# The way back from tokens to channels: 32x32 block transposes on VectorE in place of TensorE transposes, with x1 kept in another order of pixels

## The chip, the cores and the metric

The kernel runs on one core of a Trainium2 chip. The metric is the device time of one execution in microseconds (us). Before the change three runs took 6061.84, 6062.12 and 6064.63 us, median 6062.12. Five engines work side by side, each through a queue of its own in order: TensorE (PE in the profile; its weight loads are listed apart as PEld), VectorE (DVE), ScalarE (ACT), GpSimd (POOL) and SyncE (SP), which here issues the transfers. Semaphores tie them together: an instruction at the head of a queue that waits holds up everything behind it on its engine.

## The reference

The input is x, 32 images of 128 channels and 64x64 pixels, fp32. What is computed, cut to what matters:

```python
# layer 0: group norm, then a convolution by learned butterfly transforms
xc = complex(group_norm(x))
x_f = butterfly_along_h(butterfly_along_w(xc))      # 64-point transforms
prod = einsum('bihw,oihw->bohw', x_f, w_f)          # channels mixed at each frequency
x1 = x + real(inverse_butterflies(prod))

# layer 1: every pixel is a token of 128 channels
t = x1.reshape(B, C, H*W).transpose(0, 2, 1)
k, v = ln(t) @ Wk.T + bk, ln(t) @ Wv.T + bv          # ln: layer norm over channels
probs = softmax(einsum('sbe,sbf->sef', k, v) / sqrt(seq_len), axis=-1)
t = t + einsum('sef,sbf->sbe', probs, ln(t))         # one 128x128 matrix per image
p = softmax(ln(t) @ router_w + router_b)             # 8 experts, the best 2 are kept
t = t + sum(gate_of_the_two * (ln(t) @ expert_w[e] + expert_b[e]))
out = t.transpose(0, 2, 1).reshape(B, C, H, W)
```

The last line is the way back to channels.

## The kernel before

The kernel has three parts. Part one normalizes and transforms each image along w and h and writes the frequencies to DRAM (`xf`). Part two mixes channels, one column of frequencies after another, and writes `pf` to DRAM. Part three (lines 763 to 1390, from about 2600 us to the end) does all the rest, image by image, and the change lies there. 4096 pixels of an image make 32 tiles of 128 tokens, taken four at a time as groups g = 0 to 7.

For each image b, part three does the following. The names are those of the code and the profile.

- *Loads*, on SP's queue: eight tiles `r` of 256 KB from `pf` (line 856) and the image x itself, 2 MB (line 850, `y` in the profile).
- *Inverse transform.* Eight times PE makes `pu` in PSUM (line 877) and four ACT copies bring it into `u` (line 887); then PE makes `py` in four parts (line 899). `pu` and `py` share one PSUM buffer (room "cv"). For images 0 and 1 the same is done in smaller pieces in other buffers. For each `py`, `h_out` on DVE (line 907) adds PSUM to x in place. This makes x1, channels by pixels.
- *Front.* PE turns x1 into tokens, four 128x128 transposes per group into `pt` (line 1021); ACT copies `pt` into `tk[b % 2]` (line 1026), tokens by channels; DVE takes `bn_stats` (line 993) and combines them (moments, lines 1003 to 1008); POOL raises the variance to the power -1/2 (line 1013); a Gram matrix `pg` over all tokens (line 1072) and a softmax give the matrix of the attention; PE multiplies x1 by it (`pp`, line 1145), ACT scales, DVE adds to `tk` (line 1173).
- *Gate chain*, on DVE: router logits, the two largest, their weights (`logits1`, then `nmr2`, `logits2`, `first_max` twice, `second`, `between`, `gates`; lines 1204 to 1248, the last row is line 1248). It waits for a second power on POOL and has one exponential on ACT.
- *Experts*, for each group: ACT normalizes (`xn`, line 1273), PE turns (`px`, line 1283), ACT copies (`xT`, line 1289). For each of the 32 tiles two matmuls `pe` of 128x512 (line 1296; three PSUM buffers; the profile has two records for each) give eight experts' outputs; DVE multiplies each by the gates (`gated`, line 1307, here called m0_0, m0_1, ... by tile and half) into `tm` (two buffers, each a pair of tiles); POOL sums the experts and adds them to `tk` (lines 1332, 1333, 1335). In the last image five pairs are added by DVE directly (line 1319).
- *Way back*, for each group: `back(g)` is four PE transposes of `tk` into `po` (line 1342), `store(g)` is one ACT copy into `so` (line 1348) and one transfer of 256 KB to the output (line 1349).

`tk` has two buffers, so that the front of image b and the experts of image b - 1 or b - 2 run at the same time.

What sets the order is the class `Plan` (lines 25 to 87). Every step is handed to it with an engine, a supposed cost in us, a due time, the steps that must come before, and rooms that it takes and frees (the counts of buffers). The due time is 114 us times a position in the image's schedule, with a shift by the kind of step from the table `SHIFT` (line 826). Plan simulates the engines as list schedulers: a free engine takes the ready step with the earliest due time for which there is room. The instructions are then issued in exactly this order. A change of a cost, an engine, a room or a dependence can so change the order of any other step.

The steps that the prediction names are: `h`/`ho` (py and h_out), `pt`/`to`/`sa` (turn, copy, statistics), `va`, `pwa`, `na` (moments, power, and what follows it), `vb`, `pwb`, `lg`, `nb`, `l2`, `f1` to `f5`, `gt` (second norm and gate chain), `pe`/`m`/`s` (expert, gated, summed), `st`/`so` (way back).

Of the kernel before, what the change touches and what calls it, by code (L numbers as in the profile page):

```python
# [10 lines left out]
F32 = mybir.dt.float32  # L11
AF = mybir.ActivationFunctionType
ALU = mybir.AluOpType
# [3 lines left out]
P = 128  # L17
# [73 lines left out]
def kernel(  # L91
# [15 lines left out]
    nc = tc.nc  # L107
# [5 lines left out]
    n = HW  # L113
# [649 lines left out]
    eps = ctx.enter_context(tc.tile_pool(name="eps", bufs=3, space=PSUM))  # L763
    cps = ctx.enter_context(tc.tile_pool(name="cps", bufs=1, space=PSUM))
    tps = ctx.enter_context(tc.tile_pool(name="tps", bufs=3, space=PSUM))
    rp = ctx.enter_context(tc.tile_pool(name="rp", bufs=10))
    xp = ctx.enter_context(tc.tile_pool(name="xp", bufs=2))
    st = ctx.enter_context(tc.tile_pool(name="st", bufs=1))
    up = ctx.enter_context(tc.tile_pool(name="up", bufs=1))
    wp = ctx.enter_context(tc.tile_pool(name="wp", bufs=2))  # L770
# [13 lines left out]
    NG = 4  # L784
# [14 lines left out]
    def prepare():  # L799
# [20 lines left out]
        nc.tensor.matmul(pe[:, 0:NE], om, prx[0][:, P + NE : QX], start=True, stop=True)  # L820
        nc.vector.tensor_scalar_mul(rws, pe[:, 0:NE], float(P))

    plan = Plan({"cv": 1, "pe": 3, "tl": 3, "r": 10, "x": 2, "xg": NG, "xn": 2, "xT": 2, "tm": 2, "so": 2, "gate": 2})
    SLOT = 114.0

    SHIFT = {
        "ad": -0.15, "at": -0.25, "f": 0.71, "gs": -1.97, "gt": 0.71, "h": -0.24, "ho": -3.5, "kvp": 3.43,
        "kvq": -0.45, "l": 0.71, "lg": 3.61, "m": -0.32, "na": -1.87, "nb": -0.81, "pb": -1.97, "pc": -1.97,
        "pe": 0.16, "pg": -0.08, "pp": 0.19, "pr": -1.97, "prx": -1.97, "pt": -0.23, "pwa": -1.87, "pwb": 3.61,
        "px": 0.15, "r": -0.04, "s": 0.08, "sa": 1.29, "sm": -1.97, "sn": -1.97, "so": 2.13, "sr": -1.97,  # L830
        "st": 1.1, "t": -1.97, "to": 0.06, "va": -1.87, "vb": 3.61, "w": 0.28, "x": -0.68, "xT": -0.68,
        "xg": 0.21, "xn": 2.42,
    }
    made = {}
# [7 lines left out]
            engine, us, SLOT * at, run, [made[k] for k in names if k[0] >= 0], take, free, late  # L842
        )

    xs, rs, tile_of, first = {}, {}, {}, [prepare]

    def transfers(b):
        def load_x():
# [22 lines left out]
    def conv(b):  # L871
# [21 lines left out]
        def h_inverse(g):  # L893
# [7 lines left out]
                        )  # L901
            return run

        def h_out(g):
            def run():
                acc = xs[b][:, :, 16 * g : 16 * g + 16]
                nc.vector.tensor_tensor(
                    acc, tile_of.pop(("cy", b, g)).rearrange("o (w h) -> o h w", h=n), acc, ALU.add
                )
            return run  # L910


# [30 lines left out]

        def h_out_piece(q):
            def run():
                acc = xs[b][:, :, 8 * q : 8 * q + 8]
                nc.vector.tensor_tensor(
                    acc, tile_of.pop(("cz", b, q)).rearrange("o (w h) -> o h w", h=n), acc, ALU.add
                )
            return run  # L950

        if b < 2:
            for e in range(8):
                at = b + 0.08 * e
                for oh in range(2):
                    add(
                        b, f"w{e}_{oh}", "PE", 0.95, at + 0.04 * oh, w_inverse_piece(e, oh),
                        [f"r{e}"] + [(b - 1, f"h{k}") for k in range(4)], ("pe",), ("r",) if oh else (),
                    )
                    add(  # L960
                        b, f"wo{e}_{oh}", "ACT", 0.65, at + 0.04 * oh, w_out_piece(e, oh), [f"w{e}_{oh}"], (), ("pe",),
                    )
            for g in range(4):
                for k in range(2):
                    at = b + 0.68 + 0.07 * g + 0.035 * k
                    h, ho = (f"h{g}", f"ho{g}") if k else (f"h{g}_0", f"ho{g}_0")
                    add(
                        b, h, "PE", 1.05, at, h_inverse_piece(2 * g + k),
                        [f"wo{e}_{oh}" for e in range(8) for oh in range(2)] + ([f"h{g}_0"] if k else []), ("pe",),
                    )  # L970
                    add(b, ho, "DVE", 0.7, at, h_out_piece(2 * g + k), [h, "x"] + ([f"ho{g}_0"] if k else []), (), ("pe",))
            return
        for e in range(8):
            at = b + 0.08 * e
# [6 lines left out]
        for g in range(4):  # L981
            at = b + 0.68 + 0.07 * g
            add(b, f"h{g}", "PE", 2.05, at, h_inverse(g), [f"wo{e}_{oh}" for e in range(8) for oh in range(2)], ("cv",))
            add(b, f"ho{g}", "DVE", 1.2, at, h_out(g), [f"h{g}", "x"], (), ("cv",))

    def front(b):

# [27 lines left out]
        def turn(g):  # L1015
            def run():
                ps = tile_of["pt", b, g] = tps.tile([P, 512], F32, tag="tl", name=f"pt{b}_{g}")
                x1 = xs[b].rearrange("c h w -> c (h w)")
                for k in range(4):
                    i = 4 * g + k  # L1020
                    nc.tensor.transpose(ps[:, k * P : (k + 1) * P], x1[:, i * P : (i + 1) * P], ident)  # L1021
            return run
# [16 lines left out]
        s1 = b + 1  # L1039
        for g in range(8):  # L1040
            at = s1 + 0.016 * g
            add(b, f"pt{g}", "PE", 0.48, at, turn(g), [(b - 2, f"st{g}")] + [f"ho{k}" for k in range(4)], ("tl",))
            add(b, f"to{g}", "ACT", 0.55, at, turned(g), [f"pt{g}"], (), ("tl",))
            add(b, f"sa{g}", "DVE", 0.85, at, stats1(g), [f"to{g}"] + (["sa0"] if g else []))
        add(b, "va", "DVE", 1.7, s1 + 0.14, lambda: moments(1), [f"sa{g}" for g in range(8)])
# [92 lines left out]

        def product(lo, m):
            def run():  # L1140
                x1 = xs[b].rearrange("c h w -> c (h w)")
                ps = tile_of["pp", b, lo] = tps.tile([P, 512], F32, tag="tl", name=f"pp{b}_{lo}")
                for k in range(m):
                    i = lo + k
                    nc.tensor.matmul(  # L1145
                        ps[:, k * QX : (k + 1) * QX], x1[:, i * P : (i + 1) * P], prx[b % 2], start=True, stop=True
                    )
            return run
# [28 lines left out]
        for j, lo in enumerate(range(0, NT, 3)):  # L1177
            m = min(3, NT - lo)
            at = s1 + 0.45 + 0.016 * j
            add(b, f"pp{lo}", "PE", 0.26 * m, at, product(lo, m), ["prx", (b - 1, "lg")], ("tl",), ("x",) if lo == 30 else ())  # L1180
            add(
                b, f"at{lo}", "ACT", 0.4 * m + 0.2, at, scaled(lo, m),
                [f"pp{lo}"] + (["at0"] if lo else []),
            )
            add(
                b, f"ad{lo}", "DVE", 0.54 * m, at, added(lo, m),
                [f"at{lo}"] + (["ad0"] if lo else [f"pg{g}" for g in range(8)]), (), ("tl",),
            )
# [75 lines left out]
    def experts(b):  # L1264
# [70 lines left out]
                    nc.gpsimd.tensor_tensor(t[:, lo : lo + 2, :], t[:, lo : lo + 2, :], tm[:, :, m, :], ALU.add)  # L1335
            return run

        def back(g):
            def run():
                ps = tile_of["po", b, g] = tps.tile([P, 512], F32, tag="tl", name=f"po{b}_{g}")  # L1340
                for k in range(4):
                    nc.tensor.transpose(ps[:, k * P : (k + 1) * P], t[:, 4 * g + k, :], ident)
            return run

        def store(g):
            def run():
                so = wp.tile([P, 512], F32, tag="so", name=f"so{b}_{g}")
                nc.scalar.copy(so, tile_of.pop(("po", b, g)))
                nc.sync.dma_start(ov[b][:, g * 512 : (g + 1) * 512], so)
            return run  # L1350

        s2 = b + 2
        for g in range(8):
            at = s2 + 0.125 * g
            add(b, f"xn{g}", "ACT", 1.65, at - 0.1, normal(g), ["nb"], ("xn",))
            add(b, f"px{g}", "PE", 0.48, at - 0.05, turn(g), [f"xn{g}"], ("tl", "xT"), ("xn",))
            add(b, f"xT{g}", "ACT", 0.55, at - 0.05, turned(g), [f"px{g}"], (), ("tl",))
            for k in range(4):
                i = 4 * g + k
                for half in range(2):  # L1360
                    add(
                        b, f"pe{i}_{half}", "PE", 0.86, at + 0.125 * (2 * k + half) / 8, expert(i, half), [f"xT{g}"],
                        ("pe",), ("xT",) if k == 3 and half else (),
                    )
                    add(
                        b, f"m{i}_{half}", "DVE", 1.45 if i // 2 in direct else 0.64, at + 0.125 * (2 * k + half) / 8,
                        weighed(i, half) if i // 2 in direct else gated(i, half),
                        [f"pe{i}_{half}", "gt"] + ([f"m{i - k % 2}_0"] if k % 2 or half else []),
                        ("tm",) if k % 2 == 0 and half == 0 and i // 2 not in direct else (),
                        ("pe",) + (("gate",) if i == NT - 1 and half else ()),  # L1370
                    )
                if k % 2 and i // 2 in direct:
                    made[b, f"s{i // 2}"] = made[b, f"m{i}_1"]
                elif k % 2:
                    add(
                        b, f"s{i // 2}", "POOL", 5.5, at + 0.125 * (2 * k + 2) / 8, summed(i // 2),
                        [f"m{i - 1 + a}_{h}" for a in range(2) for h in range(2)], (), ("tm",),
                    )
            add(b, f"st{g}", "PE", 0.48, at + 0.25, back(g), [f"s{2 * g}", f"s{2 * g + 1}"], ("tl",))
            add(b, f"so{g}", "ACT", 0.55, at + 0.25, store(g), [f"st{g}"], (), ("tl",))  # L1380

    for b in range(B):
        transfers(b)
# [60 lines left out]
```

## Time and profile before

| | |
|---|---|
| profiled execution, span | 6062.4 us |
| median of three runs | 6062.12 us |
| PE busy | 5891.6 us, 97% |
| DVE, ACT, POOL busy | 4221.2, 3756.5, 4191.0 us |
| `po` transposes on PE (line 1342) | 155.0 us, 1024 records |
| `so` copies on ACT (line 1348) | 144.4 us, 256 |
| stores `out_dram<-so` | 256 of 256 KB, 2.2 us from issue to landing |
| loads `l<-xf` (part two, pieces of 512 B) | 1012 of 128 KB, 3.2 us |
| loads `r<-pf` | 504 of 256 KB, 4.7 us |
| load of x, `y<-in_x_dram` | 32 of 2 MB, 9.3 us |

The profile gives one span for the profiled execution, 6062.4 us, and no other time for it; it stands 0.3 us above the median of the runs. A row of a group reads: line, engine, operation, output<-input, size, count, then busy time in us and mean ns of one, then the idle time of the engine just ahead of these instructions and what ended most of it. In a time line the first number is the start in us and the second the duration; a bracket holds the idle time before it and its releaser. Matmuls are pipelined, so their durations overlap, and the time that one costs PE is better read from start to start.

### The profile page before, as it was taken

What the parts mean: (1) busy time and instruction counts of PE and PEld (TensorE: products, weight loads), DVE (VectorE), ACT (ScalarE), POOL (GpSimd) and SP (SyncE); (2) the same over time, 40 slices, a digit from 0 to 9 for tenths busy, and PEclk for the clock granted to TensorE, in tenths of its full rate; (3) what the DMA queues carried; (4) which work ended last, traced back from release to release, by engine and by line L of the source; (5) the groups of instructions that cost most, each with busy time, mean ns of one, the idle gap of its engine ahead of it and who ended that gap; (6) DMA issues with size and microseconds to landing.
All of it is one profiled execution on the core that took longest, in us unless ns stands there. A gap on an engine that the chain in (4) does not pass through costs nothing.

```text
span 6062.4 us, 219265 instructions
## 1 busy us (share of the span) xinstructions
PE 5891.6 (97%) x95372; PEld 4677.6 (77%) x95372; DVE 4221.2 (70%) x7696; ACT 3756.5 (62%) x7057; POOL 4191.0 (69%) x3765
## 2 busy tenths in 40 slices
PE   7999999999999999889999999999999999999998
PEld 7999999999999999776666666666666666666654
DVE  5565545555555555448878787787878878787878
ACT  7666664555555555366667667666766766676663
POOL 2110006666666666428898898989989898998988
PEclk9999999999999999999999999999999999999999
DMA  6767666666666666632313222231322223132100
GB/s 200 238 224 237 234 214 193 172 173 172 172 174 171 171 171 172 160 107 77 92 56 102 67 88 81 72 97 57 101 68 84 84 64 104 57 97 71 65 27 28
DMA packets 555044, 756.74 MB, mean 125 GB/s; under 512 B 58592, under 2 KB 319712, under 8 KB 549984
## 3 DMA queue, kind: packets, MB, share of 16 engines
q1 hardware_dynamic: 551856, 738.76, 41.0%
q8 instruction: 749, 12.27, 0.9%
q0 software_dynamic: 896, 2.62, 0.1%
q14 instruction: 215, 1.76, 0.1%
q10 hardware_dynamic: 1328, 1.32, 0.1%
HBM read 406.93 MB, written 335.54 MB: 122 GB/s over the span
## 4 chain that ended last, share of the span: by engine, by line
PE 88%; ACT 7%; issue 2%; DVE 1%; POOL 1%; DMA 1%; SPq 0%; ACTq 0%; POOLq 0%; DVEq 0%
PE pe L1296 28%; PE m L654 17%; PE g L632 9%; PE pf L418 7%; PE pu L877 6%; PE pp L1145 4%; PE py L899 4%; PE pg L1072 4%; PE pv L396 3%; PE px L1283 2%; ACT xn L1273 2%; ACT u L887 2%; PE pz L373 1%; PE pt L1021 1%; ACT z L383 1%
## 5 line engine op out<-in xcount | busy, mean ns | idle before, releaser
L1296 PE MATMUL pe<-ew_sb,xT 128*128 128x512 f32 x4096 | 1948.4, 597 | 18.6 <-DVE tm L1307 15.1
L1307 DVE TENSOR_TENSOR tm<-pe,oh 128x512 f32<-128x512 f32 x2028 | 1346.6, 684 | 478.9 <-PE pe L1296 456.6
L1332 POOL TENSOR_TENSOR tm<-tm 128x512 f32<-128x512 f32 x1014 | 1285.0, 1284 | 202.6 <-DVE tm L1307 199.3
L1296 PEld LDWEIGHTS pe<-ew_sb,xT 128*128 128x128 f32 x4096 | 701.6, 191 | 523.4 <-issue 400.1
L643 DVE COPY f<-g 128x1024 f32<-128x1024 f32 x508 | 622.3, 1225 | 644.4 <-PE g L632 644.2
L654 PE MATMUL m<-f,s 128*64 128x64 f32 x32768 | 1068.9, 224 | 1.1 <-ACT f L643 0.8
L654 PEld LDWEIGHTS m<-f,s 128*64 128x64 f32 x32768 | 999.0, 138 | 62.4 <-issue 1.5
L600 POOL COPY s<-l 128x512 f32<-128x512 f32 x512 | 547.2, 1105 | 526.4 <-issue 509.7
L643 ACT COPY f<-g 128x1024 f32<-128x1024 f32 x508 | 514.7, 1013 | 556.4 <-PE g L632 530.1
L1335 POOL TENSOR_TENSOR tk<-tk,tm 128x256 f32<-128x256 f32 x1014 | 753.9, 743 | 79.5
L1333 POOL TENSOR_TENSOR tm<-tm 128x512 f32<-128x512 f32 x507 | 650.3, 1283 | 39.8
L887 ACT COPY u<-pu 64x512 f32<-64x512 f32 x960 | 556.3, 579 | 135.1 <-PE pu L877 121.6
L632 PE MATMUL g<-c,wst 9*128 9x128 f32 x16256 | 599.6, 283 | 1.7 <-issue 1.5
L632 PEld LDWEIGHTS g<-c,wst 9*128 9x128 f32 x16256 | 503.0, 186 | 36.2 <-issue 1.5
L349 POOL TENSOR_TENSOR grstd<-gms,mhalf 128x1 f32<-128x1 f32 x32 | 17.8, 555 | 737.8 <-DVE gms L345 737.8
L1158 ACT ACTIVATE pp<-pp,m 128x128 f32<-128x128 f32 x1024 | 440.9, 431 | 124.2 <-PE pp L1145 99.2
L602 POOL TENSOR_SCALAR s<-l 128x512 f32<-128x512 f32 x256 | 511.3, 1997 | 0.0
L877 PEld LDWEIGHTS pu<-qw,r 128*128 128x128 f32 x3840 | 455.1, 193 | 62.8 <-ACT u L887 49.0
L877 PE MATMUL pu<-qw,r 128*128 128x128 f32 x3840 | 475.8, 277 | 25.1 <-ACT u L887 25.1
L1289 ACT COPY xT<-px 128x512 f32<-128x512 f32 x256 | 150.2, 587 | 563.2 <-PE px L1283 560.1
L418 PE MATMUL pf<-ph,v 128*128 128x128 f32 x4096 | 491.2, 278 | 6.2 <-issue 1.4
L418 PEld LDWEIGHTS pf<-ph,v 128*128 128x128 f32 x4096 | 467.0, 192 | 16.0 <-ACT z L383 7.1
(169 smaller groups left out, 8569.6 us busy)
## 6 DMA issues: line engine op xcount, KB each, us to landing
xf<-f SPq DMA_DIRECT2D x512, 256.0 KB, 3.3
pf<-o SPq DMA_DIRECT2D x1024, 128.0 KB, 3.3
l<-xf SPq DMA_DIRECT2D x1012, 128.0 KB, 3.2
r<-pf SPq DMA_DIRECT2D x504, 256.0 KB, 4.7
x<-in_x_dram SPq DMA_DIRECT2D x256, 256.0 KB, 4.5
y<-in_x_dram SPq DMA_DIRECT2D x32, 2048.0 KB, 9.3
out_dram<-so SPq DMA_DIRECT2D x256, 256.0 KB, 2.2
tw<-in_tw_dram SPq DMA_DIRECT2D x6, 384.0 KB, 7.5
```

The source lines that it names most:

```text
L418: nc.tensor.matmul(pl[:, j * P : (j + 1) * P], vs[b][:, 8 * g + j, :], ph.rearrange("h r m -> h (r m)"), start=True, stop=True,)
L600: nc.gpsimd.tensor_copy(dst, src)
L632: nc.tensor.matmul(pg[g // 2][:, g % 2, m * P : (m + 1) * P], wst[rows, 16 * half + 4 * t + m, :], c[rows].rearrange("r h k -> r (h k)"), ...
L643: copy(f.rearrange("i m (g o) -> i m g o", g=2), tile_of["g", w, half, t][k].rearrange("i g (o m) -> i m g o", o=4))
L654: nc.tensor.matmul(ps[hh * n : (hh + 1) * n, q, :], s[:, h].rearrange("i k b -> i (k b)")[:, B * r : B * r + n], f[:, h, r, :], start=(r = ...
L877: nc.tensor.matmul(ps[:, k, :], rs[b, e][:, k * P : (k + 1) * P], qw.rearrange("w r m -> w (r m)"), start=True, stop=True,)
L887: nc.scalar.copy(u[r * n : (r + 1) * n, :, oh * n + 8 * e : oh * n + 8 * e + 8], ps[oh * n : (oh + 1) * n, :, r * n : (r + 1) * n].rearran ...
L1296: nc.tensor.matmul(ps, tile_of["xT", b, i // 4][:, i % 4, :], ew_sb[:, es, :].rearrange("d e c -> d (e c)"), start=True, stop=True,)
L1307: nc.vector.tensor_tensor(tile_of["tm", b, i // 2][:, i % 2, es, :], tile_of.pop(("pe", b, i, half)).rearrange("p (e c) -> p e c", c=P), t ...
L1332: nc.gpsimd.tensor_tensor(tm[:, k, 0:4, :], tm[:, k, 0:4, :], tm[:, k, 4:8, :], ALU.add)
L1333: nc.gpsimd.tensor_tensor(tm[:, :, 0:2, :], tm[:, :, 0:2, :], tm[:, :, 2:4, :], ALU.add)
L1335: nc.gpsimd.tensor_tensor(t[:, lo : lo + 2, :], t[:, lo : lo + 2, :], tm[:, :, m, :], ALU.add)
```

## The change

x1 is no longer made in place. `h_out` writes into a new tile `y`, two buffers, in the order [16 l, 2 wh, 4 a, 32 w], where the row of a pixel is h = 16 a + l and its column 32 wh + w. A tile of 128 tokens then holds four rows, 16 apart, of 32 pixels each, so that the 32 tokens of each block of partitions are 32 neighbouring pixels. `pt` and `pp` read `y`. The x tile has one buffer in place of two and is free after the last `h_out`; `r` has seven buffers in place of ten. The four `h_out` of an image are now ordered one after another.

`back(g)` and its ACT copy are gone. `flip(g)` is one DVE instruction that transposes 32x32 blocks of four tiles of `tk` into `so`, 128x512. Four transfers of 64 KB store it, one for each block of 32 partitions, with pieces of 512 B where one transfer had rows of 2 KB. In the planner `so` is now a step of DVE that takes the room "so", `os` is the step of SP that issues the stores, the shifts of `st` and `so` (1.1 and 2.13) are replaced by 0, and `pt` of image b waits for `so` of image b - 2. Over the kernel, 1024 PE transposes and 256 ACT copies go; 256 DVE transposes come, and 1024 stores in place of 256.

```diff
-    rp = ctx.enter_context(tc.tile_pool(name="rp", bufs=10))
-    xp = ctx.enter_context(tc.tile_pool(name="xp", bufs=2))
+    rp = ctx.enter_context(tc.tile_pool(name="rp", bufs=7))
+    xp = ctx.enter_context(tc.tile_pool(name="xp", bufs=1))
+    yp = ctx.enter_context(tc.tile_pool(name="yp", bufs=2))
...
-    plan = Plan({"cv": 1, "pe": 3, "tl": 3, "r": 10, "x": 2, ...
+    plan = Plan({"cv": 1, "pe": 3, "tl": 3, "r": 7, "x": 1, "y": 2, ...
...
-        ... "so": 2.13, ... "st": 1.1, ...
+        ... "so": 0.0, "os": 0.0, ...
...
+        def added(ps, lo, m):
+            if lo == 0:
+                ys[b] = yp.tile([P, 16, 2, 4, 32], F32, tag="y", name=f"x1_{b}")
+            wh, j = divmod(lo, 32)
+            nc.vector.tensor_tensor(
+                ys[b][:, :, wh, :, j : j + m].rearrange("o l a w -> o a l w"),
+                ps.rearrange("o (w a l) -> o a l w", a=4, w=m),
+                xs[b][:, :, lo : lo + m].rearrange("o (a l) w -> o a l w", a=4), ALU.add,
+            )
+
         def h_out(g):
             def run():
-                acc = xs[b][:, :, 16 * g : 16 * g + 16]
-                nc.vector.tensor_tensor(
-                    acc, tile_of.pop(("cy", b, g)).rearrange("o (w h) -> o h w", h=n), acc, ALU.add
-                )
+                added(tile_of.pop(("cy", b, g)), 16 * g, 16)
             return run
...
-            add(b, f"ho{g}", "DVE", 1.2, at, h_out(g), [f"h{g}", "x"], (), ("cv",))
+            add(
+                b, f"ho{g}", "DVE", 1.2, at, h_out(g), [f"h{g}", "x"] + ([f"ho{g - 1}"] if g else []),
+                ("y",) if g == 0 else (), ("cv",) + (("x",) if g == 3 else ()),
+            )
...
-                x1 = xs[b].rearrange("c h w -> c (h w)")
+                x1 = ys[b].rearrange("c l v a w -> c (l v a w)")
...
-            add(b, f"pt{g}", "PE", 0.48, at, turn(g), [(b - 2, f"st{g}")] + [f"ho{k}" for k in range(4)], ("tl",))
+            add(b, f"pt{g}", "PE", 0.48, at, turn(g), [(b - 2, f"so{g}")] + [f"ho{k}" for k in range(4)], ("tl",))
...
-        def back(g):
-            def run():
-                ps = tile_of["po", b, g] = tps.tile([P, 512], F32, tag="tl", name=f"po{b}_{g}")
-                for k in range(4):
-                    nc.tensor.transpose(ps[:, k * P : (k + 1) * P], t[:, 4 * g + k, :], ident)
+        def flip(g):
+            def run():
+                so = tile_of["so", b, g] = wp.tile([P, 4, 4, 32], F32, tag="so", name=f"so{b}_{g}")
+                nc.vector.transpose(
+                    out=so.rearrange("p k t w -> p t k w"),
+                    in_=t[:, 4 * g : 4 * g + 4, :].rearrange("p t (k c) -> p t k c", c=32),
+                )
             return run
 
         def store(g):
             def run():
-                so = wp.tile([P, 512], F32, tag="so", name=f"so{b}_{g}")
-                nc.scalar.copy(so, tile_of.pop(("po", b, g)))
-                nc.sync.dma_start(ov[b][:, g * 512 : (g + 1) * 512], so)
+                so = tile_of.pop(("so", b, g)).rearrange("p k t w -> p k (t w)")
+                for a in range(4):
+                    nc.sync.dma_start(
+                        ov[b][:, a * 1024 + g * P : a * 1024 + (g + 1) * P].rearrange("(k c) m -> c k m", c=32),
+                        so[32 * a : 32 * a + 32],
+                    )
             return run
...
-            add(b, f"st{g}", "PE", 0.48, at + 0.25, back(g), [f"s{2 * g}", f"s{2 * g + 1}"], ("tl",))
-            add(b, f"so{g}", "ACT", 0.55, at + 0.25, store(g), [f"st{g}"], (), ("tl",))
+            add(b, f"so{g}", "DVE", 0.62, at + 0.25, flip(g), [f"s{2 * g}", f"s{2 * g + 1}"], ("so",))
+            add(b, f"os{g}", "SP", 0.2, at + 0.25, store(g), [f"so{g}"], (), ("so",), 4.0)
```

## The prediction

> **What bounds the kernel now.** I read the page first: its share of busy time, its chain, its groups.
>
> ```profile
> span 6062.4 us, 219265 instructions
> PE 5891.6 (97%) x95372; PEld 4677.6 (77%) x95372; DVE 4221.2 (70%) x7696; ACT 3756.5 (62%) x7057; POOL 4191.0 (69%) x3765
> ...
> PE 88%; ACT 7%; issue 2%; DVE 1%; POOL 1%; DMA 1%; SPq 0%; ACTq 0%; POOLq 0%; DVEq 0%
> ...
> L1296 PE MATMUL pe<-ew_sb,xT 128*128 128x512 f32 x4096 | 1948.4, 597 | 18.6 <-DVE tm L1307 15.1
> ```
>
> TensorE (PE) is busy throughout and carries 88% of the chain; in the last part its expert matmuls have waited only 15.1 us in all for a gated product. Three runs gave 6061.84 to 6064.63, median 6062.12; the profiled span is 0.3 us above that median, so sums against either agree.
>
> Then the last part: the last gate instruction of two images in a row (start, duration), and the same stretch by engine (length, then busy time of PE, PEld, DVE, ACT, POOL, then granted clock, DMA share, GB/s).
>
> ```profile
> 3971.40 0.43 DVE L1248 TENSOR_TENSOR oh<-oh,tops 128x256 f32<-128x256 f32 x1
> 4077.76 0.43 DVE L1248 TENSOR_TENSOR oh<-oh,tops 128x256 f32<-128x256 f32 x1
> ```
>
> ```profile
> 4000.00:4106.37 106.37, 105.03 (x746) 71.82 (x744) 85.48 (x190) 73.01 (x168) 95.24 (x83) 1.00 0.25 80
> ```
>
> An image costs 106.36 us; PE is idle for 1.34 of it, POOL works 95 and DVE 85. DMA at a quarter is no bound. Third, the groups of what goes (busy, mean ns, idle before), and PE's time line around two of them.
>
> ```profile
> L1342 PE MATMUL po<-ident,tk 128*128 128x128 f32 x1024 | 155.0, 274 | 8.0 <-POOL tk L1335 7.4
> L1348 ACT COPY so<-po 128x512 f32<-128x512 f32 x256 | 144.4, 591 | 129.6 <-PE po L1342 126.2 <-DMA out_dram<-so 1.5 <-ACT xn L1273 1.1
> ```
>
> ```profile
> 4070.44 0.60 PE L1021 MATMUL pt<-ident,y 128*128 128x128 f32 x4
> 4070.87 0.60 PE L1342 MATMUL po<-ident,tk 128*128 128x128 f32 x4
> 4071.31 1.02 PE L1296 MATMUL pe<-ew_sb,xT 128*128 128x512 f32 x2
> 4072.17 0.60 PE L1021 MATMUL pt<-ident,y 128*128 128x128 f32 x4
> ```
>
> Durations overlap, so I price PE from start to start: four transposes 0.44 us, one expert matmul (two records) 0.86; likewise pu 1.79, py 2.02.
>
> **What comes off.** Per image 8 x 0.44 = 3.5 us of PE leave, 113 us in 32 images. The 8 ACT copies (144 us in all) go as well; ACT is busy 73 of 106 us an image, so they are worth nothing by themselves.
>
> **What comes on.** (a) Eight flips an image on DVE. No row shows a 32x32 transpose. A 128x512 product out of PSUM starts 0.60 us after the one before; 1.37 us is the longest that a 128x256 row (L1220) took while POOL worked on SBUF. I take 0.62, near the row of the same size, and keep 0.6 to 1.4: 5 to 11 us an image, in 21 us of DVE idleness. (b) Four stores instead of one per group: SP issues at 0.34 us, so 1.35 a group, 10.8 an image of 106. The 512 B pieces are those of the loads l (128 KB, 3.2 us to landing); so is written again no sooner than about 10 us later. I cost it at zero; the r loads behind these issues on SP are 0.6 of a period early, and that cover would have to go first. (c) x1 into y: h_out reads the same PSUM stride and still writes runs of 16 pixels, so 1.2 us as now (ends 1.14, its pitch, and 2.4, if the fourth dimension doubled it, which would put 2.4 us on each boundary, 53 in all). One x buffer: its load starts when ho3 is over, about 85 us before the next use, and takes 9.3; zero. Seven r buffers: zero by the same early issue. (d) pt of image b now waits for the flip of b-2 on DVE, no longer for PE's own po.
>
> **What moves.** The planner writes the whole order anew, and here lies the price. I read the changed program's order at the boundary between images (E is the end of the last expert matmul). From boundary 6 to 27 it is always the same. PE: last expert matmul, py_2, py_3, two px, three pe (all that the three PSUM buffers hold), pu_0, pt_7, pu_1, pu_2, then the fourth pe, which needs the first gated product of the new image (m0_0). DVE: last m, then the whole gate chain (L1224 to L1260) with no expert product inside, and between its links two h_out, flip 7, the bn statistics of pt_7's group and the moments; then m0_0. In the kernel before, m28 to m31 lie inside that chain, so PE has expert work meanwhile.
>
> The unmixed chain has a price in the trace: before's own last boundary lets it run almost so. Its first link starts at 5876.10, its last ends at 5891.30: 15.2 us. What PE does there:
>
> ```profile
> 5877.53 3.16 PE L1283 MATMUL px<-ident,xn 128*128 128x128 f32 x8 [2.98 <-ACT xn L1273]
> 5880.69 5.49 PE L1296 MATMUL pe<-ew_sb,xT 128*128 128x512 f32 x6
> ...
> 5892.14 4.93 PE L1296 MATMUL pe<-ew_sb,xT 128*128 128x512 f32 x6 [5.05 <-DVE tm L1307]
> ```
>
> Three expert matmuls, then a wait of 5.05 us for DVE: this is the picture I expect at every boundary. Six records take 2.74 us in the steady stretch; here, after waits of 2.98 and 5.05, they took 5.49 and 4.93.
>
> DVE from E: last m 0.65, chain 15.2, two h_out 2.4, flip 0.62, statistics 0.85, moments 0.8, m0_0 0.6: 21.1 us. PE in that time: py 2 x 2.02, px 2 x 0.44, pe 3 x 0.86, pu 3 x 1.79, pt 0.44: 13.3. Idle 7.8 us, in three or four pieces (before h_out frees the one "cv" buffer; before each next pu, whose four ACT copies take 2.4; before the fourth pe). The change gains as long as this is under 3.5 + 1.3 = 4.8.
>
> Idle so costs clock as well. Where pu stood alone between copies, the trace shows
>
> ```profile
> 2679.48 2.05 PE L877 MATMUL pu<-qw,r 128*128 128x128 f32 x16 [2.44 <-ACT u L887]
> 2683.97 3.38 PE L877 MATMUL pu<-qw,r 128*128 128x128 f32 x16 [2.44 <-ACT u L887]
> ```
>
> ```profile
> 2680.00:2682.00 2.00, 1.53 (x14) 1.34 (x12) 1.86 (x5) 0.43 (x1) 2.00 (x1) 1.00 0.44 139
> ...
> 2684.00:2686.00 2.00, 2.00 (x11) 2.00 (x12) 1.72 (x6) 2.00 (x6) 0.11 (x1) 0.61 0.60 195
> ```
>
> The second line has a granted clock of 0.61, and its pu took 1.33 us more, after gaps of 2.44. Not each gap does it (the first pu kept 1.00); I take one and a half such losses a boundary, 2.0 us, with ends 0 and 3.4 (a loss after the pu chain and the smaller of the two above after the last wait would be 3.5).
>
> The Trainium skill, "TensorE: Matmul & The Clock Gate", section "HAM oscillation", asks only that PE not idle for more than about 3.4 us; by that rule gaps of 2.4 keep the clock and the time would be 44 us lower, 6168. The row above contradicts it. "VectorE: DVE Perf Modes", section "Rules for kernel authors", sends a 128x128 transpose to TensorE where PSUM will do, which speaks against the change, and its table "The three transpose paths" gives bf16 390 ns there and 311 ns for the blocks on VectorE; estimated from it, a flip is 4 x 311 = 1.24 us, 14 us more in all than my sum. The trace has 0.44 us for four in fp32 on PE; no run here yet shows the other.
>
> Sum of one image: 105.0 - 3.5 + 7.8 + 2.0 = 111.3 us, +4.9; 22 boundaries: +108. Boundaries 0 to 2 have more pu behind the three pe (+1 each, 3), 3 to 5 as the steady ones with the power of the moments on POOL inside the chain as well (5.44 us, about 2 of it uncovered; +7 each, 21). Around 28 to 30 little inverse work is left to fill (+5 each, 15). At the end, flips that wait for POOL and one flip with four issues in place of po, copy and one issue (+3). Together +150: 6212 us.
>
> **Rivals.** *A, other side: the idle is filled and PE's work simply comes off.* 97% PE speaks for it, the order against it. It decides where DVE brings m0_0 within 18.1 us of E. Then 6062 - 113 = 5949; POOL, 97.8 us an image from 16 sums of 5.43 and two powers of 5.44, allows 102.9. *B: the flip is slow.* At 1.4 us only one flip lies on the chain, +0.8 x 22 = 18 and some delay of products: about 6235; at 3 us it passes what three PSUM buffers cover (2.6 us), seven more each some 0.4 an image: about 6320. Against it: the 0.60 us row. *C: idle, but the clock stays.* 6062 + 22 x 2.9 + 38 = 6164. For it: the pu of 2679.48. *D: stores land late and flips wait.* Decides only over 10 us of landing, against 3.2 shown; each us beyond costs DVE, not PE, up to the 21 us idle; under 6230.
>
> **How the numbers follow.** Main case 0.62, C 0.13, B with D 0.11, A 0.10, something between A and the rest, near 6062, 0.04. Predicted 6212. Main case's ends: the small gate rows vary with POOL (L1220 424 ns median, 1376 at most), so a chain shorter by 1.3 us and no clock loss gives 22 x 1.6 + 30 = 6127; idle 8.8, clock 3.4 and 2 us of waits after the boundary, where POOL's first sum starts late, give 22 x 9.3 + 45 = 6312. The range 6100 to 6310 holds main and C almost whole and half of B. What a measurement here can tell from no change is about 0.2%, 12 us. Slower by more: 0.86 (main, C, B); within: 0.03; faster: 0.11 (A and a little).
>
> **What would show it.** No L1342 and L1348; PE's share falls to about 93%. The last gate row comes every 111 us. The wait of pe for tm grows from 15 to over 60 us, that of pu for ACT's u from 25 to over 80, and the granted clock dips once an image. Flip rows of 0.6 us. I am wrong if the period is under 106.4, if the gate chain of the new order takes much under 15 us, or if PE's idle at boundaries is under 5.

## The result and the profile after

The changed kernel takes 6356.07 us, median of four runs (6351.7 to 6361.2), against 6062.44 us for the kernel before in the same measurement. The ratio is 1.0485, with a 95% interval of 1.047 to 1.050. Slower was forecast, at 6212 us within 6100 to 6310. The direction held, and the loss is almost twice the forecast one: 294 us instead of 150.

The page of the changed kernel: the span, the shares of the engines, the chain that ended last, and the two groups of PE that wait.

```profile
span 6352.2 us, 218090 instructions
PE 5900.7 (93%) x94348; PEld 4639.8 (73%) x94348; DVE 4351.1 (68%) x7952; ACT 3609.7 (57%) x6801; POOL 4179.1 (66%) x3765
...
PE 78%; DVE 12%; ACT 5%; issue 2%; POOL 2%; DMA 1%; SPq 0%; ACTq 0%; DVEq 0%; POOLq 0%
...
L1308 PE MATMUL pe<-ew_sb,xT 128*128 128x512 f32 x4096 | 1976.1, 606 | 133.7 <-DVE tm L1319 121.1
...
L878 PE MATMUL pu<-qw,r 128*128 128x128 f32 x3840 | 528.0, 296 | 145.7 <-ACT u L888 137.7
```

PE fell from 97% to 93%, and DVE's share of the chain rose from 1% to 12%. The wait of the expert matmuls for DVE went from 15.1 to 121.1 us, that of pu for ACT's copies from 25.1, in the row of the kernel before that follows, to 137.7.

```profile
L877 PE MATMUL pu<-qw,r 128*128 128x128 f32 x3840 | 475.8, 277 | 25.1 <-ACT u L887 25.1
```

PE's busy time has not fallen by the 113 us that were taken off it; it rose by 9, while the granted clock of the whole run fell from 0.99 to 0.975.

The last gate row of an image comes every 116.0 us in the steady stretch, where it came every 106.4. The two rows below are from the time line of DVE, and the third is the same period by engine (length, then busy time of PE, PEld, DVE, ACT, POOL, then granted clock, DMA share, GB/s).

```profile
4093.60 0.43 DVE L1260 TENSOR_TENSOR oh<-oh,tops 128x256 f32<-128x256 f32 x1
...
4209.71 0.42 DVE L1260 TENSOR_TENSOR oh<-oh,tops 128x256 f32<-128x256 f32 x1
```

```profile
4093.60:4209.71 116.11, 105.71 (x713) 71.39 (x712) 90.31 (x198) 68.49 (x159) 95.04 (x83) 0.97 0.26 73
```

PE is idle for 10.4 us of this image instead of 1.3, and busy 105.7 instead of 105.0, although 3.5 us of work are gone. That is 4.2 us more than what was left (105.0 less 3.5), at a granted clock of 0.97; the rows below show 3.3 of them as rows that ran longer behind gaps. Taking the distances of the gate rows of both kernels, the 289.8 us between the two spans divide as follows: boundaries 6 to 27 cost 195 (most 9.6 each, 8.9 in the mean), 3 to 5 cost 55, 0 to 2 cost 27, 28 to 30 cost 24; the start of the last part and the last image give 11 back. The worst single one is boundary 3, with 132.3 us, in part at a granted clock of 0.83:

```profile
3130.00:3150.00 20.00, 12.68 (x122) 11.23 (x120) 5.44 (x20) 11.06 (x22) 14.73 (x9) 0.83 0.37 102
```

How the steady boundary looks is seen in the time line of PE behind the last expert matmul of an image, which ends at 4076.24 (start, duration, what, idle time before it and its releaser).

```profile
4076.24 2.09 PE L900 MATMUL py<-hm,u 128*64 128x64 f32 x64
4079.66 2.08 PE L900 MATMUL py<-hm,u 128*64 128x64 f32 x64 [1.33 <-DVE x L909]
...
4083.00 2.84 PE L1308 MATMUL pe<-ew_sb,xT 128*128 128x512 f32 x6 [0.24 <-ACT xT L1301]
4086.64 2.05 PE L878 MATMUL pu<-qw,r 128*128 128x128 f32 x16 [0.80 <-DVE x L909]
...
4091.76 3.68 PE L878 MATMUL pu<-qw,r 128*128 128x128 f32 x16 [2.63 <-ACT u L888]
4097.88 3.13 PE L878 MATMUL pu<-qw,r 128*128 128x128 f32 x16 [2.44 <-ACT u L888]
4100.80 3.36 PE L1308 MATMUL pe<-ew_sb,xT 128*128 128x512 f32 x6
```

The idle pieces sum to 7.4 us. After gaps of 2.63 and 2.44 us the two pu took 3.68 and 3.13 us instead of 2.05, and the six records of pe 3.36 instead of 2.74. The fourth expert matmul comes 24.6 us after the last one of the image before. Its buffer had been free for some 6 us: m0_0 started at 4094.13 and took 0.68.

The other 3.0 us of idle time lie ahead of the boundary. The chain of work that ended last leaves PE there and runs through DVE (selected pieces, start, duration, what):

```profile
4166.21 0.88 PE pe L1308 x2
...
4173.41 1.23 DVE m L1016
...
4174.77 1.19 DVE m L1018
...
4177.35 0.62 DVE so L1353
...
4180.31 1.38 DVE lg L1218
4181.69 1.44 DVE eq L1219
...
4186.01 1.13 PE pe L1308 x2
```

Between the expert products stand the moments, a flip and the router logits, and the expert matmuls wait for the products behind them. Rows that take 0.2 or 0.4 us elsewhere take 1.2 to 1.4 here, beside GpSimd's sums: the row of L1016 ends at 4174.64, a sum on POOL at 4174.57. The last section comes back to this.

### The profile page after: what moved, and what is told of

It is laid out like the page before. It is cut to its first block, busy times and chain, and to the rows that moved or that the text cites. A ratio compares the mean times of both kernels' runs of the same rounds, so it can differ in the third digit from the quotient of the medians.

```text
span 6352.2 us, 218090 instructions
## 1 busy us (share of the span) xinstructions
PE 5900.7 (93%) x94348; PEld 4639.8 (73%) x94348; DVE 4351.1 (68%) x7952; ACT 3609.7 (57%) x6801; POOL 4179.1 (66%) x3765
## 4 chain that ended last, share of the span: by engine, by line
PE 78%; DVE 12%; ACT 5%; issue 2%; POOL 2%; DMA 1%; SPq 0%; ACTq 0%; DVEq 0%; POOLq 0%
PE pe L1308 22%; PE m L654 16%; PE g L632 9%; PE pu L878 7%; PE pf L418 6%; PE pg L1084 4%; PE pp L1157 4%; DVE tm L1319 3%; PE pv L396 3%; PE py L900 2%; ACT u L888 2%; DVE bs L1005 2%; PE px L1295 1%; PE pz L373 1%; ACT z L383 1%
## 5 line engine op out<-in xcount | busy, mean ns | idle before, releaser
L1308 PE MATMUL pe<-ew_sb,xT 128*128 128x512 f32 x4096 | 1976.1, 606 | 133.7 <-DVE tm L1319 121.1
L1319 DVE TENSOR_TENSOR tm<-pe,oh 128x512 f32<-128x512 f32 x2028 | 1332.8, 681 | 523.3 <-PE pe L1308 483.4
L1308 PEld LDWEIGHTS pe<-ew_sb,xT 128*128 128x128 f32 x4096 | 715.5, 194 | 711.1 <-issue 435.4
L878 PEld LDWEIGHTS pu<-qw,r 128*128 128x128 f32 x3840 | 503.0, 209 | 229.5 <-ACT u L888 159.0
L878 PE MATMUL pu<-qw,r 128*128 128x128 f32 x3840 | 528.0, 296 | 145.7 <-ACT u L888 137.7
L1025 POOL TENSOR_TENSOR m<-m,mhalf 128x32 f32<-128x32 f32 x64 | 351.3, 5489 | 320.9 <-DVE m L1020 320.9
L1005 DVE BATCH_NORM_STATS2 bs<-tk 128x6 f32<-128x128 f32 x2048 | 449.6, 279 | 59.7 <-ACT tk L1038 47.2
```

The costliest lines, as they stand in the source:

```text
L878: nc.tensor.matmul(ps[:, k, :], rs[b, e][:, k * P : (k + 1) * P], qw.rearrange("w r m -> w (r m)"), start=True, stop=True,)
L1005: nc.vector.bn_stats(bs[:, i].rearrange("p a s -> p (a s)"), t[:, i, :])
L1308: nc.tensor.matmul(ps, tile_of["xT", b, i // 4][:, i % 4, :], ew_sb[:, es, :].rearrange("d e c -> d (e c)"), start=True, stop=True,)
L1319: nc.vector.tensor_tensor(tile_of["tm", b, i // 2][:, i % 2, es, :], tile_of.pop(("pe", b, i, half)).rearrange("p (e c) -> p e c", c=P), t ...
```

## Experiments

Two theories stood against each other. The first: the operations cost little, and the order that the planner wrote for them is what loses. The second: the flips, the stores or the buffers cost by themselves.

### The new pixels, buffers and stores with the old way back

x1 in y, the x buffer, the r buffers and four stores a group stay; PE transposes and ACT copies come back.

```diff
+                ps = tile_of["po", b, g] = tps.tile([P, 512], F32, tag="tl", name=f"po{b}_{g}")
+                for k in range(4):
+                    nc.tensor.transpose(ps[:, k * P : (k + 1) * P], t[:, 4 * g + k, :], ident)
...
+                nc.scalar.copy(
+                    so, tile_of.pop(("po", b, g)).rearrange("c (t a w) -> c a t w", t=4, a=4)
+                )
                 for a in range(4):
                     nc.sync.dma_start(
...
+                        ov[b][:, a * 1024 + g * P : a * 1024 + (g + 1) * P],
+                        so[:, a].rearrange("c t w -> c (t w)"),
                     )
...
+            add(b, f"st{g}", "PE", 0.48, at + 0.25, back(g), [f"s{2 * g}", f"s{2 * g + 1}"], ("tl",))
+            add(b, f"so{g}", "ACT", 0.55, at + 0.25, store(g), [f"st{g}"], (), ("tl",))
```

> The new order of pixels, x1 in y, one x buffer, seven r buffers and four stores of 64 KB with 512 B pieces stay; the way back is again four PE transposes and one ACT copy per group (the copy puts the pixels in order), and the planner is given the steps of before. Theory 1: 6062 within 0.3%, since none of this is on PE's path. Rival (the buffers, h_out's new writes or the stores cost): slower than 6080.

Measured: 6055.62 us, ratio 0.9994 (0.9985 to 1.0004). In the old order nothing of this costs anything, the 512 B pieces and the four times as many issues included; a store lands in 1.6 us. That part of the second theory is out.

### The flips in the order of before

The planner is given the steps of before, and where they stood the flip and the stores are issued. The steps of PE, DVE, ACT and POOL come out in exactly the order of before; on SP only the loads of x move.

```diff
-            add(b, f"so{g}", "DVE", 0.62, at + 0.25, flip(g), ..., ("so",))
-            add(b, f"os{g}", "SP", 0.2, at + 0.25, store(g), [f"so{g}"], (), ("so",), 4.0)
+            add(b, f"st{g}", "PE", 0.48, at + 0.25, flip(g), ..., ("tl",))
+            add(b, f"so{g}", "ACT", 0.55, at + 0.25, store(g), [f"st{g}"], (), ("tl",))
```

> The change's own operations in the order of the kernel before: the planner is given the old steps (a step of PE and one of ACT per group), and where they stood the flip and the stores are issued. PE, DVE, ACT and POOL then have the steps of before in the same order, with the flip where the four transposes were planned. Theory 1 (the loss is made by the new order, not by the operations): the transposes come off PE and the flips lie in DVE's idle time, so not slower than before, between 5950 (all of PE's 113 us gained) and 6060; the gate chain keeps its expert products. Rival (the flip, its stores or the new order of pixels cost by themselves): slower than 6062, toward 6356.

Measured: 6159.22 us, ratio 1.0166 (1.0149 to 1.0183). Theory 1 as it was put, not slower than before, is out. The rival's wording, slower and toward 6356, is met, but only a third of the way: 100 us of the 294, against 6059.63 us for the kernel before in the same measurement. So the old order recovers two thirds of the loss, and of the rival's three causes the run above leaves the flips alone. A look at a stretch tells why. It begins with the second expert product behind the first logits and ends with the first h_out behind the end of the gate chain. In both kernels it holds the same VectorE instructions, but for seven of the image's eight flips; first the kernel before, then this one:

```profile
4160.01:4194.84 34.83, 33.49 (x244) 23.92 (x243) 32.55 (x74) 26.57 (x54) 28.25 (x26) 1.00 0.46 137
```

```profile
4407.17:4444.99 37.82, 32.58 (x215) 21.73 (x214) 34.96 (x82) 23.00 (x46) 28.84 (x27) 0.95 0.45 127
```

The kernel before has DVE busy for 32.6 of 34.8 us in just that stretch, nearly as densely as PE; its idle time lies elsewhere. Here the stretch is 3.0 us longer, which is what an image loses (109.3 us against 106.4). Most of it appears right behind the gate chain, where two flips stand before a product that PE waits for:

```profile
4435.02 2.07 PE L1308 MATMUL pe<-ew_sb,xT 128*128 128x512 f32 x2 [2.60 <-DVE tm L1319]
```

### Both orders without the flips

The flip is cut down to one element per partition, with its waits and stores kept, once in the order of before and once in the order of the changed kernel.

```diff
-                nc.vector.transpose(
-                    out=so.rearrange("p k t w -> p t k w"),
-                    in_=t[:, 4 * g : 4 * g + 4, :].rearrange("p t (k c) -> p t k c", c=32),
-                )
+                nc.vector.tensor_copy(so[:, 0, 0, 0:1], t[:, 4 * g + 3, P - 1 : P])
```

> The kernel with the flips in the order of before, each flip cut down in the same way. It tells what it is worth to take the transposes off TensorE and the copies off ScalarE, with nothing put on VectorE. Theory 2 (after the run with the order of before: VectorE sets the pace around the boundary, and five of the eight flips lie there): 6159 falls by some 5 x 0.65 x 31 = 100 us, to 6040 to 6075, and PE's 113 us are hardly gained at all. Rival (TensorE bounds the kernel, as its 97% say): 5950 to 5980.

Measured: 6051.44 us, ratio 0.9975 (0.9966 to 0.9985). So in that order the flips cost 108 us (6159.22 less 6051.44, from two measurements in which the kernel before took 6059.63 and 6064.87). Taking 113 us of transposes off PE and 144 us of copies off ACT is worth 13 us (9 to 21 by the interval), with 0.14 us of each flip left on DVE. PE's share of 97% did not mean that PE alone set the pace. In the same stretch DVE stays dense, and PE, which was idle for 1.3 us of it in the kernel before, is now idle for 3.1:

```profile
4261.34:4295.51 34.17, 31.06 (x216) 20.90 (x215) 32.89 (x81) 23.17 (x47) 28.93 (x27) 1.00 0.51 140
```

> The changed kernel in its own order, each flip cut down to a copy of one element per partition into a fixed tile of zeros, so that its waits and its stores stay and only its 0.70 us of VectorE go (the output is zeros but for these elements). Theory 1 (the planned order costs): in the chain of the changed kernel only one or two flips an image lie on the path, 0.6 to 1.3 us, so 6315 to 6356. Rival (the flips' time on VectorE costs): 8 x 0.63 an image come back, 6180 to 6220.

Measured: 6355.98 us, ratio 1.0475 (1.0457 to 1.0492). In the changed kernel the flips cost nothing that can be measured: the same 6356 with and without them. So its loss is not made by the flips' time on VectorE; their waits and their stores are still in it. Its PE still waits for the copies and for DVE with the flips cut down:

```profile
4103.19 2.95 PE L881 MATMUL pu<-qw,r 128*128 128x128 f32 x16 [2.63 <-ACT u L891]
4108.58 3.79 PE L881 MATMUL pu<-qw,r 128*128 128x128 f32 x16 [2.44 <-ACT u L891]
4189.25 1.12 PE L1311 MATMUL pe<-ew_sb,xT 128*128 128x512 f32 x2 [1.67 <-DVE sos L1356]
```

Another run on the same question left the flips out and stored tk itself.

> The changed kernel with its planned order kept, but the flips are left out: the stores send tk as it stands, so the output holds blocks that are not transposed. Theory 1: DVE loses 5.6 us an image (8 rows of 0.70), but DVE was not late at the boundary; 6356 falls by no more than 40 us. Rival (the flip's time on DVE is what costs): falls by over 100 us, toward 6200 or less.

Measured: 6519.79 us, ratio 1.0756 (1.0740 to 1.0772), slower than both theories allow. It did not test them: a store that reads tk holds the tile until it has landed, and the ACT copies of the next image into tk waited 345.9 us for it in all.

```profile
L1038 ACT COPY tk<-pt 128x512 f32<-128x512 f32 x256 | 149.1, 586 | 629.2 <-DMA out_dram<-tk 345.9 <-PE pt L1033 244.0 <-POOL tk L1347 22.2
```

### The flips moved to where DVE is idle

The order of before again; flips 0 to 6 are issued behind the first product of the second next pair.

```diff
+                early = half == 0 and i % 4 == 2 and i >= 6 and b < B - 1
...
+                if early:
+                    flip(i // 4 - 1)()
+                    store(i // 4 - 1)()
```

> The change's operations in the order of before, as in the first run, but flips 0 to 6 of an image (the last image excepted) are issued on VectorE right behind the first product of the second next pair, which has waited for the sum of that group anyway. Five of the eight flips so leave the last 30 us of the period, in which VectorE was busy 26.1 of 26.6 us, for its first 75, in which it had idle time. Theory 2 (VectorE's time in that stretch is what the flips cost): 5 x 0.65 x 31 = 100 us come back, 6055 to 6090. Rival (the flips wait for something wherever they stand, or cost by their number): 6130 to 6160, as in the first run.

Measured: 6073.12 us, ratio 1.0012 (1.0003 to 1.0021). Of the 100 us that were lost in that order, all but 8 are gone (against 6064.90 us for the kernel before in the same measurement), with the same number of flips. The 26.1 of 26.6 us of the expectation are the last 26.6 us before the gate row in the run without the move. The stretch of the first comparison, with two flips left in it, is short again, while DVE's whole image grew to 91 us:

```profile
4270.40:4304.84 34.44, 30.32 (x215) 20.89 (x214) 33.39 (x76) 23.13 (x46) 28.39 (x27) 1.00 0.35 104
```

This shows the place to be what a flip costs. It also is the whole change at the time of before: with the old order and seven flips moved in it, the time is that of before within 0.2%. So the order, and not the operations, makes the changed kernel slow.

### The fourth expert matmul first

In the changed kernel the fourth pe stands behind pu_1 and pu_2, 6 us after its buffer is free. This run moves it ahead, at 22 boundaries. In the code w1 and w2 are the steps of pu_1 and pu_2, and pe1_1 is the fourth pe.

```diff
+        for j in range(6, 28):
+            at = pe.index(made[j, "pe1_0"])
+            last = pe.index(made[j, "pe1_1"])
+            pus = [i for i in pe[at:last] if i in (made[j + 3, "w1"], made[j + 3, "w2"])]
+            for i in pus:
+                pe.remove(i)
+            for i, after in zip(pus, ("pe1_1", "pe2_1")):
+                pe.insert(pe.index(made[j, after]) + 1, i)
```

> The changed kernel, with one edit of the order on TensorE at 22 boundaries (the images 6 to 27): the fourth expert matmul goes ahead of pu_1 and pu_2, and pu_2 behind two more. Theory (the fourth pe is late because it stands behind two pu that wait for ScalarE's copies, 6 us after its gated product has freed a buffer): 2 to 4 us a boundary less, 6270 to 6310. Rival (the copies of pu_1 and pu_2 then come late on ScalarE, whose queue has the next image's normalization behind them): 6356 or slower, up to 6420.

Measured: 6444.83 us, ratio 1.0623 (1.0607 to 1.0638). It is slower by 89 us. The theory is out; the rival had the direction, but the time lies 25 us above its upper end. PE now idles 5.75 us for the first product, where it had made two pu before, and the pu still wait for each other's copies afterwards:

```profile
4122.90 2.07 PE L1308 MATMUL pe<-ew_sb,xT 128*128 128x512 f32 x2 [5.75 <-DVE tm L1319]
4130.43 2.05 PE L878 MATMUL pu<-qw,r 128*128 128x128 f32 x16 [0.72 <-ACT u L888]
4134.93 2.05 PE L878 MATMUL pu<-qw,r 128*128 128x128 f32 x16 [2.44 <-ACT u L888]
```

Moving this one wait did not help: PE waits for the product in place of the copies. Whether other work could have filled the stretch was not run.

### A wholly new order

The planner's costs and due times are set anew, by kind of step and by step, in three tables that are not shown.

```diff
+        at += SHIFT.get(kind, 0.0) + MORE.get(kind, 0.0) + (EACH.get(key, 0.0) if b > 1 else 0.0)
+        us *= COST.get(kind, 1.0)
```

> The changed kernel, all its operations, with another order: the planner's costs and due times are set anew, by kind of step and by step, so that the gate chain has expert products between its links again and the flips lie where VectorE is idle. Nothing else differs. Theory (the change loses by its order alone): PE's 101.5 us an image and 1 to 3 us of idle, 2 to 4 us an image less than before's 106.4, 5930 to 6010. Rival (VectorE or GpSimd bound it whatever the order): 6050 or more.

Measured: 6305.12 us, ratio 1.0396 (1.0379 to 1.0414). The theory missed: 51 us better than the changed kernel, far from 6010. The rival's number, 6050 or more, is met here and by the run with early flips, but 6305 is no such bound, since that run does the same operations in 6073. Whether VectorE or GpSimd bounds the change near 6050 stays open. What this order got wrong is seen in its DVE: 94.2 us busy an image with the very same rows that took 90.3 in the changed kernel.

```profile
4284.80:4398.00 113.20, 103.42 (x713) 68.20 (x712) 94.20 (x198) 69.23 (x161) 95.12 (x83) 1.00 0.26 75
```

The last three gate rows of this kernel with POOL beside them, and then the same three rows of the changed kernel:

```profile
4393.81 2.50 POOL L1773 TENSOR_TENSOR tm<-tm 128x512 f32<-128x512 f32 x2 [0.59 <-DVE tm L1748]
...
4395.42 1.17 DVE L1687 TENSOR_TENSOR oh<-oh,tops 128x256 f32<-128x256 f32 x1
4396.38 1.33 POOL L1774 TENSOR_TENSOR tm<-tm 128x512 f32<-128x512 f32 x1
4396.62 1.38 DVE L1688 TENSOR_TENSOR oh<-oh,oh 128x256 f32<-128x256 f32 x1
4397.80 0.80 POOL L1776 TENSOR_TENSOR tk<-tk,tm 128x256 f32<-128x256 f32 x1
4398.04 0.84 DVE L1689 TENSOR_TENSOR oh<-oh,tops 128x256 f32<-128x256 f32 x1
```

```profile
4092.43 5.44 POOL L1025 TENSOR_TENSOR m<-m,mhalf 128x32 f32<-128x32 f32 x1 [7.30 <-DVE m L1020]
...
4092.75 0.36 DVE L1258 TENSOR_TENSOR oh<-oh,tops 128x256 f32<-128x256 f32 x1
4093.14 0.42 DVE L1259 TENSOR_TENSOR oh<-oh,oh 128x256 f32<-128x256 f32 x1
4093.60 0.43 DVE L1260 TENSOR_TENSOR oh<-oh,tops 128x256 f32<-128x256 f32 x1
```

Beside POOL's sums, such a row ends 0.28 us after the POOL instruction that is running ends; beside POOL's power it takes its own 0.36 to 0.43 us. Over all images the three rows have medians of 1.17, 1.38 and 0.84 us in this order, and of 0.36, 0.42 and 0.42 in the changed kernel. The new order put these rows and more of the moments beside the sums. An order that allows for this was not run, and whether one exists that beats the kernel before stays open.

## Why the prediction was right and wrong

**What comes off.** Nearly right as an amount, and wrong as a worth. In the old order with the flips cut down, PE is busy 102.1 us an image where it was 105.0. The step that PE's idle time bounds what the change can bring (3.5 and 1.3 us) treated PE as the only engine on the path. With all the transposes and copies gone and 0.14 us in the place of each flip, the old order gains 13 us, not 113.

**What comes on.** The flip was taken at 0.62 us and measures 0.70, or 0.62 from start to start; stores, y, x and r were costed at zero, and the run with the old way back confirms it. Rivals B and D are out. From the price that the Trainium skill gives in "VectorE: DVE Perf Modes", section "The three transpose paths", for a bf16 128x128, the prediction had worked out an estimate of 1.24 us for a flip; the measurement decides, and is about half of it. The flips were costed against "21 us of DVE idleness" in an image. That reading failed: in the old order the flips cost 108 us, because the stretch of 34.8 us where seven of them stood had 2.3 us of that idleness. It is not what took the forecast off, since in the changed kernel the flips' time cost nothing.

**What moves.** The reading of the new order was right, and the order is the cause: with the flips cut down the changed kernel takes the same 6356 us, and the same operations in the old order, with seven flips moved, take 6073. The idle time at the boundary was worked out as 7.8 us and measures 7.4, and that is partly luck. DVE was put at 21.1 us from E to the end of m0_0 and took 18.5. The 15.2 us taken for the chain already held statistics, the moments and a wait of 1.81 us for a copy, and the sum added statistics and moments once more. Against PE's 13.3 us, 18.5 would leave 5.2 idle if the fourth pe waited for m0_0 alone. It came at 24.6, held by two pu and their ACT copies ahead of it in PE's queue. So m0_0 came close to the 18.1 us at which rival A was to decide, and A still did not hold. One row was misread as well: of L1220 in the kernel before, 1376 ns is the median and 424 the least, so the slow rows beside POOL were the rule and not the exception.

**The sum of one image.** It gave 111.3 us against 116.0, and two mis-sized terms make up the difference. The clock was put at 2.0 us, with an upper end of 3.4, and PE's work took 4.2 more than it should, of which 3.3 show in the rows: both pu after gaps of 2.4 to 2.6 us ran slow, and the expert matmuls behind them as well. The Trainium skill's rule, in "TensorE: Matmul & The Clock Gate", section "HAM oscillation", asks for no idle gaps of PE over about 3.4 us. These rows stayed below that and slowed all the same, as the row in the prediction had. And the likeliest case had no waits outside the boundary, where 3.0 us appeared: DVE was dense from 4166 to 4186 with statistics, moments, a flip and logits between the expert products, and some of these rows were held beside POOL's sums. The working had a wait of 2 us only at its upper end, and gave the late start of POOL's first sum as the reason. The 22 boundaries cost 195 us in place of 108.

**The other boundaries.** 0 to 2 were put at 3 us and cost 27, 3 to 5 at 21 and cost 55, 28 to 30 at 15 and cost 24. Here the working put a figure on each without walking through its instructions. Boundary 3 shows the same gaps and a lower clock; what the others lose in detail was not looked at and stays open. The tail was put at 3 us; the start of the last part and the last image gave 11 back.

**The range.** It ended at 6310, from the upper ends of the steady case, 22 boundaries of 9.3 us or 205 in all, with 45 us for all else. The steady case came out near that end, 195 us in all, but within it. All else came out at 95. So the steady terms make most of the miss of the likeliest value, and the other boundaries carried the time out of the range.

## What to carry to other kernels

An engine's idle time in an image is no room for new work unless it lies where the work will stand: cost it by the stretch in which it must run. Where two engines are dense in the same stretch, taking work off one of them may give almost nothing, even at 97%: here 13 us of 113. And where a planner writes the order, a change of a few steps is a change of the whole program: run the new operations in the old order to tell one from the other.

## What the runs showed of the hardware

- VectorE's element-wise rows whose inputs both lie in SBUF wait for GpSimd's tensor instruction in progress. Rows of 0.36 to 0.43 us took 0.84 to 1.38 us beside the sums. The moments, six rows twice an image (L1444 to L1449 of the new order), took 4.8 and 2.6 us there, where the changed kernel takes 3.5 and 0.9. The Trainium skill, in "GPSIMD Engine Reference", section "8. Key points", names such contention for instructions with two SBUF inputs or in a 2-port mode and gives no size there. In these runs a scalar-operand row of the moments was held too (1.27 us against 0.18), while reductions (0.42), reciprocals (0.35), statistics (0.28), flips (0.70) and the products that read PSUM (0.68) kept their time, and GpSimd's power of 5.44 us held nothing.
- Over 20 us of boundary 3 of the changed kernel, with gaps of PE of 1.3 to 2.6 us, the granted clock was 0.83.
- A store of 64 KB in pieces of 512 B landed in 1.6 to 1.8 us in the median, one of 256 KB with rows of 2 KB in 2.2; four of the small in place of one cost nothing in the old order.
